# Second batch's expert blocks sorted on the chip by first tile; its output tiles added and stored between later blocks

## The chip, the cores and the metric

One Trainium2 chip, one core. The metric is the device time of the kernel in microseconds; before the change it is 1344.52 (median of 3 runs, 1341.7 to 1344.9). TensorE (PE in the profile) does matrix products, VectorE (DVE) and ScalarE (ACT) elementwise work, GpSimd (POOL) issues indirect DMAs here, and SyncE (SP) issues most of the plain DMAs.

## What is computed

Two layers over two images of 256 channels and 56 x 56 pixels, so N = 3136 tokens per batch. The first is a linear-attention convolution block; the second is causal attention and a mixture of experts. Only the last part is touched:

```python
def _L1_ffn_ref(x, gate_w, gate_b, W1, b1, W2, b2):
    xf = x.reshape(-1, Dd)
    logits = xf @ gate_w + gate_b
    probs = jax.nn.softmax(logits, axis=-1)
    top2_vals, top2_idx = jax.lax.top_k(probs, 2)
    cw = jnp.zeros((N, Ee), dtype=xf.dtype).at[jnp.arange(N)[:, None], top2_idx].add(top2_vals)
    def step(acc, params):
        w1, bb1, w2, bb2, we = params
        h = jax.nn.gelu(xf @ w1 + bb1, approximate=False)
        y = h @ w2 + bb2
        return (acc + we[:, None] * y, None)
    out, _ = jax.lax.scan(step, jnp.zeros_like(xf), (W1, b1, W2, b2, cw.T))
    return out.reshape(Bb, Tt, Dd)
...
t = t + _L1_ffn_ref(_ln_t(t), ...)
x = _from_tokens(t, x)
```

There are 8 experts, of hidden width 512. Each token goes to two experts, and the two outputs are added with their weights to the token. The result is written with channels ahead of pixels, so each tile of 128 tokens is transposed.

## The kernel before

**Pairs, slots, blocks.** A batch has 25 tiles of 128 tokens (the last has 64). A token with one of its experts is a pair: 6272 a batch. `dispatch(b)` (L923) works out on the chip where each pair goes: pairs are sorted by expert and, within an expert, by token, into slots; 128 slots are a block with one expert. There are 105 blocks (`NBLK`). Blocks 0 to 41 (below `FULL0`) are surely full of batch 0; blocks up to 56 (below `MIXED` = 57) may hold pairs of both; the rest is batch 1's. `dispatch` ends with a table of each block's expert (`eblks`) and of its bias (`b1bs`), L1073 to L1118, sets `ranked`, and then scatters normalised token rows into the slots in DRAM (`x_slots`) by indirect DMAs from GpSimd (L1135), 50 a batch.

**The block loop.** `experts` (L1151) runs the 105 blocks in a pipeline written out by hand: for iteration n it fetches the rows of a group of three blocks six blocks ahead (L1164, one DMA, SyncE), works out two blocks ahead where each row's result goes (`load`, L1177: `eq`, `to`), does the hidden layer of block n (L1236, L1245), the transposes of block n + 1 (L1213, L1217), copies the expert's first weights (L1224), and the output product of block n - 3 (L1255, L1265). Its result `ys` is stored by slot (`y_slots`, L1270) for blocks below 57, and scattered by token (`y_tokens`, L1272, GpSimd) for blocks from 42 on.

**Work between blocks.** At the end of each iteration `between` calls `pull`, which takes steps from jobs in a queue, the first job that has something to do first: two steps per block, three while batch 1's rows are being scattered. The jobs are `tokens` (projection, then `dispatch`), `closing` (which ends the attention's pools and runs `judge`, a check of the softmax sums), and, once block 56 has been worked, `finish(0)`. The program order of each engine is the order in which these steps are written.

**The end of a batch.** `finish(b)` (L1310) goes over 13 pairs of tiles: `fetch` gets the two experts' outputs `y0`, `y1` (for batch 0 by four indirect gathers from `y_slots`, L1334; for batch 1 by two plain loads from `y_tokens`, L1329), `add` adds them with their weights (L1349, four operations), `store` transposes (L1361), copies (L1366) and writes out (L1367; SyncE's queue for batch 0, ScalarE's for batch 1). `finish(1)` runs after all blocks, in a pool of its own, with 13 buffers. The rows it loads lie in `y_tokens` by token, and in the slot order each tile's rows come from blocks of every expert, the last expert's among them.

Of the kernel before, what the change touches and what calls it, by code (L numbers as in the profile page):

```python
# [9 lines left out]
F32 = mybir.dt.float32  # L10
U32 = mybir.dt.uint32
I32 = mybir.dt.int32
# [15 lines left out]
def conv_attn_moe_kernel(  # L28
# [18 lines left out]
    out: bass.AP,  # L47
):


# [25 lines left out]
    nc = tc.nc  # L76
# [275 lines left out]
    for c in range(NH):  # L352
# [36 lines left out]
        allow_small_or_imprecise_dtypes=True,  # L389
    )  # L390
    mixed_start = const.tile([P, E], F32, name="mixed_start")
    nc.gpsimd.iota(
# [34 lines left out]
    def layer1(nm, general):  # L427

        with ExitStack() as whole:
# [493 lines left out]
            def dispatch(b):  # L923
# [137 lines left out]
                for k in range(2):  # L1061
# [8 lines left out]
                    yield from small_piece()  # L1070


                s, e = (0, MIXED) if b == 0 else known[1]  # L1073
                if b == 1:
                    nc.vector.tensor_tensor(upto, upto, nfull.to_broadcast([P, E]), ALU.add)
                    nc.vector.tensor_scalar(upto, upto, float(E), None, ALU.add)
                past = g1.tile([P, e - s, E], F32, tag="blk", name=f"past_{nm}{b}")
                nc.vector.tensor_tensor(
                    past,
                    number[:, s:e].unsqueeze(2).to_broadcast([P, e - s, E]),  # L1080
                    upto.unsqueeze(1).to_broadcast([P, e - s, E]),
                    ALU.is_ge,
                )
                eb = g1.tile([P, e - s], F32, tag="eb", name=f"eb_{nm}{b}")
                nc.vector.tensor_reduce(eb, past, AX.X, ALU.add)
                yield from small_piece()
                if b == 0:
                    step = g1.tile([P, MIXED], F32, tag="step", name=f"step_{nm}{b}")
                    nc.vector.tensor_scalar(step, number[:, :MIXED], nfull, -float(E), ALU.is_ge, ALU.mult)
                    nc.vector.tensor_tensor(eb, eb, step, ALU.add)  # L1090
                    nc.vector.tensor_scalar(step, number[:, :MIXED], nfull, 0.0, ALU.subtract, ALU.max)
                    nc.vector.tensor_tensor(early, eb, step, ALU.add)
                    eb = early
                else:
                    nc.vector.tensor_scalar(eb, eb, float(E - 1), None, ALU.min)
                    step = g1.tile([P, MIXED - FULL0], F32, tag="step", name=f"step_{nm}{b}")
                    edge = few("edge")
                    nc.vector.tensor_scalar(edge[:, :1], nfull, float(E), None, ALU.add)
                    nc.vector.scalar_tensor_tensor(
                        step, number[:, FULL0:MIXED], edge[:, :1], early[:, FULL0:], ALU.is_lt, ALU.mult  # L1100
                    )
                    nc.vector.tensor_tensor(
                        eb[:, : MIXED - FULL0], eb[:, : MIXED - FULL0], step, ALU.add
                    )
                w = known[b][1] - known[b][0]
                nc.vector.tensor_copy(eblks[b], eb[:, :w])

                hot = g1.tile([E, w], F32, tag="hot", name=f"hot_{nm}{b}")
                nc.vector.tensor_tensor(hot, eb[:E, :w], row.to_broadcast([E, w]), ALU.is_equal)
                yield from small_piece()  # L1110
                for _ in range(1 if b else 3):
                    yield True
                bp = bank(f"bp_{b}", (P, KH, w))
                for k in range(KH):
                    nc.tensor.matmul(bp[:, k, :], b1s[:, k, :], hot, start=True, stop=True)
                nc.vector.tensor_copy(b1bs[b], bp)
                yield from small_piece()
                ranked[b] = True  # L1118
                while b and not scatter_rows:
# [31 lines left out]
            def experts(w1s, w2s, b2s, ex, es, ps6, between, need, written):  # L1151
# [4 lines left out]
                def fetch(g):  # L1156
                    s, e = g * GB, (g + 1) * GB
                    b = 0 if e <= FULL0 else 1
                    need(b)
                    if g == 0:  # L1160
                        return early_rows, None
                    f = known[b][0]
                    xb = ex.tile([P, GB, xds[b].shape[1]], F32, tag="xb", bufs=3, name=f"xb_{nm}_{g}")
                    (nc.sync if g > 2 else nc.scalar).dma_start(  # L1164
                        out=xb, in_=xds[b][(s - f) * P : (e - f) * P].rearrange("(n p) w -> p n w", p=P)
                    )
                    mixed = max(0, min(e, MIXED) - s) if b else 0
                    other = None
                    if mixed:
                        other = ex.tile([P, GB, C], F32, tag="xo", bufs=1, name=f"xo_{nm}_{g}")  # L1170
                        nc.sync.dma_start(
                            out=other[:, :mixed],
                            in_=xds[0][s * P : (s + mixed) * P].rearrange("(n p) w -> p n w", p=P),
                        )
                    return xb, other

                def load(g, xb, other):  # L1177
# [3 lines left out]
                    if b:  # L1181

                        eq = es.tile([P, GB], F32, tag="eq", name=f"eq_{nm}_{g}")
                        nc.vector.tensor_tensor(eq, xb[:, :, C + 1], slot_id[:, s:e], ALU.is_equal)
                        nc.vector.tensor_scalar(eq, eq, -float(N), float(N + OFF), ALU.mult, ALU.add)
# [64 lines left out]
                def outputs(n, state):  # L1250
# [20 lines left out]
                    if n >= FULL0:  # L1271
# [11 lines left out]
                        tc.declare_no_dep(s.ins, group=group, reason="different rows")  # L1283
                        tc.add_to_no_dep_group(group, s.ins)
                    if n == MIXED - 1:
                        written()
# [23 lines left out]
            def finish(b, oy, bufs):  # L1310
# [3 lines left out]
                def fetch(n, m, k):  # L1314

                    ys = [
                        oy.tile([P, 2, C], F32, tag=f"y{c}", bufs=bufs, name=f"y{c}_{nm}{b}_{n}")
                        for c in range(2)
                    ]
                    rows = t[:k, n : n + m, :C]  # L1320
                    if b == 0:
                        res = oy.tile([P, 2, C], F32, tag="res", bufs=bufs + 1, name=f"res_{nm}_{n}")
                        rows = res[:k, :m]
                        nc.sync.dma_start(out=rows, in_=rest_d[:k, n : n + m])
                    ahead.append((n, m, k, ys, rows))
                    for c, y in enumerate(ys):
                        r = c * N + n * P
                        if b:
                            nc.sync.dma_start(  # L1329
                                out=y[:k, :m],  # L1330
                                in_=y_tokens[r : r + (m - 1) * P + k].rearrange("(n p) d -> p n d", p=k),
                            )
                        for a in range(0 if b else m):
                            nc.gpsimd.indirect_dma_start(  # L1334
# [8 lines left out]
                            )  # L1343
                            yield True

                def add(n, m, k, ys, rows):
# [8 lines left out]
                def store(n, m, k, ys, rows):  # L1355
# [3 lines left out]
                    for o in range(NH):  # L1359
# [6 lines left out]
                    nc.scalar.copy(ot[:, :, :w], yo[:, :, :w])  # L1366
                    (nc.sync, nc.scalar)[b].dma_start(  # L1367
                        out=out[b, :, n * P : n * P + w].rearrange("(c p) n -> p c n", p=P),
# [4 lines left out]
                parts = deque(pairs())  # L1373
                while parts or ahead:
                    if parts:
                        yield from fetch(*parts.popleft())
                    if len(ahead) == bufs or not parts:
# [5 lines left out]
                        added = now  # L1383
                store(*added)

# [32 lines left out]

            projected, ranked, sent = ([False] * B for _ in range(3))
            first, early_rows, scatter_rows = [], [], []  # L1420
# [133 lines left out]
            def closing():  # L1554

                if not general:
# [5 lines left out]
                    while not projected[B - 1]:  # L1562
                        yield False
                    yield from judge()
                end.close()
# [4 lines left out]
            with ExitStack() as moe:  # L1570
# [17 lines left out]
                def need(b):  # L1588
                    while not sent[b]:
                        pull()  # L1590

                def written():
                    spread_rows.close()
                    oy = pool(moe, "oy", bufs=2, side="right")
                    queue.append(finish(0, oy, 2))

                with tc.manual_schedule(engines={PE, DVE, POOL, SP, ACT}):
                    experts(
                        first[0], w2s, b2s, ex, es, ps6,
                        lambda: pull(3 if ranked[1] and not sent[1] else 2), need, written,  # L1600
                    )
                while queue:
                    pull()
            early_w.close()
            with ExitStack() as last:
                oy = pool(last, "oz", bufs=2)
                for _ in finish(1, oy, 13):
                    pass

# [67 lines left out]
```

## Time and profile before

| | us |
|---|---|
| median of 3 runs | 1344.52 |
| profiled execution, span | 1375.5 |
| TensorE busy / VectorE / ScalarE / GpSimd | 1299.2 / 787.8 / 613.9 / 311.3 |
| block 0, copy of its transposed rows (L1217) | 884.63 |
| block 42 | 1071.35 |
| block 61 | 1142.25 |
| block 104, the last | 1321.46 |
| scatters of batch 1's rows, first and last start | 968.43, 1049.93 |
| first and last output store of batch 1, issued | 1340.73, 1370.33 |

Reading it: the copy at L1217 occurs once per block, so differences of its starts are the time of a block. A group's busy time is summed over the whole execution; the idle time beside it is that of the engine just before the group's instructions. Loads of registers and the issue of DMAs aren't counted as busy.

### The profile page before, as it was taken

The numbers are of one execution on the slowest core, as the hardware profiler recorded it, in microseconds if no ns is written. First come the engines' busy times: TensorE is split into PE (matmuls) and PEld (weight loads), VectorE is DVE, ScalarE is ACT, GpSimd is POOL, SyncE is SP. The second block draws the span as 40 slices with busy tenths as digits, with TensorE's granted clock in tenths as the row PEclk, the third lists the DMA queues.
The fourth block names the chain that finished last, engine by engine and source line by source line (L and its number), as shares of the span: only waits on it lengthen the run. The fifth ranks groups of instructions, "written<-read, shape, count | busy, mean of one in ns | idle before, by whom it ended". The sixth has DMA issues, their size and how long they took to land. (4 is left out here: it accounts for less than half of the span.)

```text
span 1375.5 us, 27937 instructions
## 1 busy us (share of the span) xinstructions
PE 1299.2 (94%) x10642; PEld 819.4 (60%) x10642; DVE 787.8 (57%) x1634; ACT 613.9 (45%) x1247; POOL 311.3 (23%) x299
## 2 busy tenths in 40 slices
PE   8999999999999999999999999999888998999973
PEld 7875444444444444434444444488878998999962
DVE  1572555757777455568587878647333443444435
ACT  0245555555565554555544565543223332343321
POOL 1113110000000221100043440000563125555530
PEclk9999999999999999999999999999999999999995
DMA  9992000000000001000011124411433334444427
GB/s 300 383 315 99 23 19 26 24 16 16 16 9 23 8 2 36 11 15 10 14 54 51 52 92 169 134 46 62 131 131 117 105 108 129 122 146 134 128 85 242
DMA packets 110373, 123.94 MB, mean 90 GB/s; under 512 B 19423, under 2 KB 99948, under 8 KB 110232
## 3 DMA queue, kind: packets, MB, share of 16 engines
q1 hardware_dynamic: 92456, 89.67, 21.5%
q0 software_dynamic: 10416, 26.00, 5.5%
q10 hardware_dynamic: 7360, 6.39, 1.4%
q8 instruction: 88, 1.44, 0.4%
q14 instruction: 53, 0.43, 0.1%
HBM read 63.04 MB, written 60.81 MB: 90 GB/s over the span
## 5 line engine op out<-in xcount | busy, mean ns | idle before, releaser
L645 ACT ACTIVATE st_f<-sc_f 128x896 f32<-128x896 f32 (+5 forms) x400 | 333.9, 838 | 291.9 <-PE sc_f L637 255.2
L659 DVE TENSOR_TENSOR acc_f<-acc_f,st_f 128x896 f32<-128x896 f32 (+5 forms) x372 | 366.6, 986 | 166.5 <-ACT st_f L645 157.9
L677 PE MATMUL yp_f<-st_f,v_f 64*64 64x448 f32 (+6 forms) x3184 | 341.0, 504 | 7.8 <-DVE qT_f L688 6.6
L637 PE MATMUL sc_f<-qT_f,kT_f 64*64 64x448 f32 (+6 forms) x3184 | 341.3, 500 | 0.0
L1236 PE MATMUL ht_f<-xT_f,w_f 128*128 128x128 f32 x1680 | 213.0, 281 | 27.0 <-ACT xT_f L1217 17.4
L1245 ACT ACTIVATE g_f<-ht_f,b1b 128x128 f32<-128x128 f32 x420 | 120.1, 369 | 265.1 <-PE ht_f L1236 158.2
L1236 PEld LDWEIGHTS ht_f<-xT_f,w_f 128*128 128x128 f32 x1680 | 206.3, 196 | 40.0 <-ACT xT_f L1217 25.2
L637 PEld LDWEIGHTS sc_f<-qT_f,kT_f 64*64 64x64 f32 x3184 | 117.1, 133 | 151.2 <-issue 136.7
L677 PEld LDWEIGHTS yp_f<-st_f,v_f 64*64 64x64 f32 x3184 | 111.3, 133 | 159.2 <-issue 131.3
L485 POOL TENSOR_SCALAR xn_f<-t 128x256 f32<-128x256 f32 (+1 forms) x50 | 67.3, 1355 | 548.1 <-issue 333.5
L1135 POOL DMA_INDIRECT x_slots<-xr_f,idx x100 | 114.1, 1141 | 247.2 <-DVE xr_f L1127 138.1
L1224 DVE COPY w_f<-w1s_f 128x1024 f32 x105 | 73.4, 699 | 94.4 <-PE ht_f L1236 47.2
L1265 DVE TENSOR_TENSOR ys_f<-yp_f,kT_f 128x128 f32<-128x128 f32 x105 | 30.6, 291 | 122.9 <-PE yp_f L1255 91.6
L1272 POOL DMA_INDIRECT y_tokens<-ys_f,to_f x63 | 63.8, 1013 | 145.3 <-DVE ys_f L1265 137.0
L523 PE MATMUL qk_f<-px_f,wat 128*128 128x512 f32 (+1 forms) x224 | 92.4, 558 | 1.2 <-ACT px_f L508 1.2
L647 DVE TENSOR_TENSOR st_f<-st_f,keep 128x256 f32<-128x256 f32 (+1 forms) x112 | 44.2, 395 | 64.8 <-ACT st_f L645 64.3
L523 PEld LDWEIGHTS qk_f<-px_f,wat 128*128 128x128 f32 x224 | 38.6, 190 | 54.3 <-issue 44.8
L1255 PE MATMUL yp_f<-px_f,g_f 128*128 x210 | 63.6, 385 | 0.0
L1255 PE MATMUL yp_f<-kT_f,g_f 128*128 x210 | 63.2, 383 | 0.0
L1255 PE MATMUL yp_f<-v_f,g_f 128*128 x210 | 62.6, 380 | 0.0
L1255 PE MATMUL yp_f<-w2s_f,g_f 128*128 x210 | 62.5, 379 | 0.0
L1334 POOL DMA_INDIRECT y_f<-y_slots,idx x50 | 56.5, 1131 | 16.3 <-issue 15.0
(217 smaller groups left out, 1177.5 us busy)
## 6 DMA issues: line engine op xcount, KB each, us to landing
x_slots<-fill SPq DMA_DIRECT2D x1, 8127.0 KB
xb_f<-x_slots SPq DMA_DIRECT2D x21, 387.0 KB
x_slots<-fill SPq DMA_DIRECT2D x1, 7296.0 KB
y_slots<-ys_f SPq DMA_DIRECT2D x57, 128.0 KB
kept<-t SPq DMA_DIRECT2D x2, 3200.0 KB
x<-in_x_dram SPq DMA_DIRECT2D x14, 448.0 KB
xr<-in_x_rows_dram SPq DMA_DIRECT2D x12, 512.0 KB
y_f<-y_tokens SPq DMA_DIRECT2D x24, 256.0 KB
```

Of the source, the lines that this page charges most:

```text
L485: nc.gpsimd.tensor_scalar(xn[:k, a], ts[b][:k, n + a, :C], ts[b][:k, n + a, MEAN : MEAN + 1], ts[b][:k, n + a, RSTD : RSTD + 1], ALU.subtr ...
L523: nc.tensor.matmul(ps[:, :w], wat[:, c, d0 : d0 + P], xT[:, c, :w], start=(c == 0), stop=(c == NH - 1),)
L637: nc.tensor.matmul(ps[h : h + HS, a, c0:W], kT[hp][rows, j * P + h : j * P + h + HS], qT[rows, hp, q0 + c0 : q0 + W], start=True, stop=True,)
L645: nc.scalar.activation(st[:k, :, c0:], ps[:k, :, c0:W], AF.Exp, scale=SCALE)
L659: nc.vector.tensor_tensor(acc[:k, :, c0:], acc[:k, :, c0:], st[:k, :, c0:], ALU.add)
L677: nc.tensor.matmul(yp[a * HS : (a + 1) * HS, h // HS, c0:W], v[hp][h : h + HS, j, a, :HS], st[h : h + HS, a, c0:], start=first, stop=bool( ...
L1135: s = nc.gpsimd.indirect_dma_start(out=xds[b], out_offset=bass.IndirectOffsetOnAxis(ap=idxs[b][:kk, k, n : n + 1], axis=0), in_=xr[:kk], i ...
L1224: nc.vector.tensor_copy(w, w1s[:, :, bass.ds(e, 1), :].rearrange("p c e h -> p c (e h)"))
L1236: nc.tensor.matmul(ht[:, k, :], w[:, c, k * P : (k + 1) * P], xT[:, c, :], start=(c == 0), stop=(c == NH - 1),)
L1245: nc.scalar.activation(g[:, k, :], ht[:, k, :], AF.Gelu, bias=b1bs[b][:, k, i : i + 1])
L1255: nc.tensor.matmul(yp[:, :C], g[:, k, :], w2s[k][:, bass.ds(e, 1), :].rearrange("p e d -> p (e d)"), start=(k == 0), stop=(k == KH - 1),)
L1272: s = nc.gpsimd.indirect_dma_start(out=y_tokens, out_offset=bass.IndirectOffsetOnAxis(ap=to[:, n % GB : n % GB + 1], axis=0), in_=ys, in_o ...
```

## The change

Four things are done.

1. `dispatch(1)` no longer builds the block table in line. It hands a job, `last_blocks`, to a list `side`, of which one step is taken per block besides the steps of `pull`, and goes on to scatter rows. `last_blocks` computes for each of the 63 blocks from 42 on the tile of its first pair, turns this into a key (blocks of the mixed region first, in their old order; blocks past the end last), ranks the keys, and permutes the table of experts. It keeps `qblk`, which place in `x_slots` the block at each position has, and `sid`, its slots' numbers.
2. The fetch of rows for batch 1 loads three places into SyncE's registers and issues three DMAs, one per block, in place of one.
3. `finish(1)` runs in the block loop, ahead of `finish(0)` in the queue, with 3 buffers. A pair of tiles is loaded when two more blocks have been worked than `complete` says; added two blocks after its load; stored a block after its adds. What is left after block 104 follows at once. The loads are declared independent of scatters of blocks that can't hold their rows. Its stores go by SyncE's queue. `pull` takes three steps per block once 57 blocks have been worked.
4. `judge` becomes a job at the end of the queue.

```diff
+def one_hot(eb, w):
+    nc.vector.tensor_copy(eblks[b], eb[:, :w])
...
+def last_blocks():
+    R = NBLK - FULL0
+    FAR = 1.0e5
...
+    nc.vector.tensor_scalar(
+        before, tot[:R].rearrange("p e t -> p (e t)"), rank, None, ALU.is_le
+    )
+    yield True
+    key, expert, own_part = (col(f"c_{k}") for k in ("key", "expert", "own"))
+    nc.vector.tensor_reduce(key, before, AX.X, ALU.add)
+    nc.vector.tensor_reduce(expert, past, AX.X, ALU.add)
+    nc.vector.scalar_tensor_tensor(key, expert, -float(NCH), key, ALU.mult, ALU.add)
...
+    keys = bank("keys", (P, 512))
+    nc.tensor.transpose(keys[:R, :R], key.to_broadcast([R, R]), ident[:R, :R])
+    less = small("one0").rearrange("p t e -> p (t e)")[:R, :R]
+    nc.vector.tensor_scalar(less, keys[:R, :R], key, None, ALU.is_lt)
+    nc.vector.tensor_reduce(rank, less, AX.X, ALU.add)
+    move = small("one1").rearrange("p t e -> p (t e)")[:R, :R]
+    nc.vector.tensor_scalar(move, number[:R, :R], rank, None, ALU.is_equal)
...
+    moved = bank("moved", (P, 2, R))
+    for k, c in enumerate((expert, own[:R])):
+        nc.tensor.matmul(moved[:, k], c.to_broadcast([R, P]), move, start=True, stop=True)
...
+    nc.vector.tensor_copy(qblk, moved[:, 1])
...
+if b == 0:
+    yield from first_blocks()
+else:
+    side.append(last_blocks())
+placed[b] = True
...
-(nc.sync if g > 2 else nc.scalar).dma_start(
-    out=xb, in_=xds[b][(s - f) * P : (e - f) * P].rearrange("(n p) w -> p n w", p=P)
-)
+if b:
+    at = nc.values_load_multi_w_load_instructions(
+        qblk[0:1, s - f : e - f], engines=(SP,), ...
+    )[1]
+    table = xds[b].rearrange("(n p) w -> n p w", p=P)
+    for a in range(GB):
+        nc.sync.dma_start(
+            out=xb[:, a],
+            in_=table[bass.ds(at[a], 1)].rearrange("o p w -> p (o w)"),
+        )
...
+def complete(n):
+    return min(NBLK, (2 * N + 2 * n * P) // P + E)
+
+def load(n, m, k):
...
+        i = nc.sync.dma_start(
+            out=y[:k, :m],
+            in_=y_tokens[r : r + (m - 1) * P + k].rearrange("(n p) d -> p n d", p=k),
+        ).ins
+        for block, other in scattered:
+            if block >= complete(n + m):
+                tc.declare_no_dep(i, other, reason="different rows")
...
-    (nc.sync, nc.scalar)[b].dma_start(
+    nc.sync.dma_start(
...
+GAP = 2
+while parts or ahead or added:
+    now = worked[0]
+    over = now == NBLK
+    if parts and len(ahead) < bufs:
+        n, m, k = parts[0]
+        if over or now >= complete(n + m) + GAP:
+            ahead.append((now, load(*parts.popleft())))
+            yield True
+            continue
+    if added and (over or now > added[0]):
+        store(*added[1])
+        added = None
+        yield True
+    elif ahead and not added and (over or now >= ahead[0][0] + GAP):
+        yield from add(*ahead[0][1])
+        added = now, ahead.popleft()[1]
+    else:
+        yield False
...
-    yield from judge()
+    queue.append(judge())
...
+def meanwhile():
+    scatters = placed[1] and not sent[1]
+    pull(3 if scatters or worked[0] >= MIXED else 2)
+    if side and next(side[0], None) is None:
+        side.popleft()
...
-with ExitStack() as last:
-    oy = pool(last, "oz", bufs=2)
-    for _ in finish(1, oy, 13):
-        pass
```

## The prediction

> **What bounds the kernel now.** I read the page's first two parts, then the engine times by stage, then the timeline of the end, then the waits of SyncE's queue there. The page's chain of waits is no help: it holds only the last three pieces, all on ScalarE and its queue. The stages say more (window, its length, then busy time of each engine with its count of instructions, the granted clock, the DMA share and GB/s):
>
> ```profile
> 1100.00:1150.00 50.00, 49.97 (x347) 46.83 (x346) 18.55 (x52) 18.30 (x66) 16.04 (x17) 1.00 0.42 128
> 1200.00:1250.00 50.00, 48.47 (x339) 44.83 (x338) 23.84 (x67) 20.19 (x68) 27.99 (x26) 1.00 0.47 143
> 1340.00:1375.50 35.50, 13.48 (x47) 7.95 (x46) 19.44 (x46) 7.30 (x13) 0.00 (x0) 0.50 0.77 245
> ```
>
> While expert blocks run, TensorE (first figure) is full and everything else has room. In the last window TensorE is idle for most of the time, at half clock, and DMA is busy 77%. So there are two limits: TensorE sets the block loop, and a chain of transfers sets the end. The timeline of the end shows that chain:
>
> ```profile
> 1331.85 0.97 POOL L1272 DMA_INDIRECT y_tokens<-ys_f,to_f  x1 [0.75 <-DVE ys_f L1265]
> 1334.67 6.65 SPq L1329 DMA_DIRECT2D y_f<-y_tokens  x10
> 1337.45 1.67 DVE L1349 SCALAR_TENSOR_TENSOR t<-y_f,wt,t 128x256 f32<-128x256 f32 x4 [5.88 <-DMA y_f<-y_tokens]
> 1338.78 1.30 PE L1361 MATMUL yo_f<-ident,t 128*128 128x128 f32 x4 [7.73 <-DVE t L1349]
> 1340.73 0.39 ACTq L1367 DMA_DIRECT2D out_dram<-ot_f  x1
> ...
> 1370.33 0.48 ACTq L1367 DMA_DIRECT2D out_dram<-ot_f  x1
> ```
>
> The last expert matmul ends at about 1331.05 (its last row starts at 1330.67 and lasts 0.38). The last scatter follows, then all 13 pairs of output tiles of batch 1 are loaded, added, transposed and stored. The first pair leaves at 1340.73, the thirteenth at 1370.33, and the span ends at 1375.50. The tail is 1375.50 - 1331.05 = 44.45 us. SyncE's queue shows why it cannot begin sooner: its first load waits for the scatters.
>
> ```profile
> SPq L1329 <- DMA y_tokens<-ys_f,to_f: 14.7, 1, 14.7
> ```
>
> In the block loop one ScalarE copy (L1217) marks each block. An undisturbed block, and then one that carries a store of batch 0:
>
> ```profile
> 1086.28 0.39 ACT L1217 COPY xT_f<-tp_f 128x256 f32<-128x256 f32 x1
> 1090.01 0.39 ACT L1217 COPY xT_f<-tp_f 128x256 f32<-128x256 f32 x1
> ...
> 1296.81 0.39 ACT L1217 COPY xT_f<-tp_f 128x256 f32<-128x256 f32 x1
> 1301.65 0.39 ACT L1217 COPY xT_f<-tp_f 128x256 f32<-128x256 f32 x1
> ```
>
> These are 3.73 us and 4.84 us.
>
> **What the Trainium skill says.** "DMA: Bandwidth & Descriptors", Anatomy of one DMA: a DMA from GpSimd has about 2.0 us of fixed cost, most of it the confirmation that the last byte has landed. The trace agrees: 2.82 us from the last scatter's start to the first load. This hop stays. The same page, Issuing engines are not separate DMA queues: all queues share 16 engines, so the output moved from ScalarE's queue to SyncE's saves no transfer time. No line here tests that alone. "TensorE: Matmul & The Clock Gate", What's actually happening: after an idle window of about 3.4 us TensorE runs at half clock. Here, the 16 hidden-layer matmuls of a block take 1.95 us, and 3.78 us after an idle of 3.06 us at 1162.24. A stall is therefore paid twice.
>
> **The change part by part.**
>
> (a) *Tail.* I followed the schedule by hand: 57 blocks are worked when both finish jobs start; a pair n, n+1 counts as complete at 49 + 2(n+2) + 8 blocks, is loaded 2 blocks later, added 2 after that, stored 1 after that. So pairs 0 to 18 (ten) are stored by block 102 of 105. Pair 20 is loaded at 103 and added and stored after the last block; pairs 22 and 24 are loaded after it. New tail, on the old time axis: the loads of pair 22 issue at 1334.67 as now, since they wait for the last scatter. Pair 20 lies in SBUF and is added and transposed in the gap of 5.88 us that VectorE now has. Pair 22 takes the place of today's first pair: out at 1340.73. Pair 24 has 64 rows and one tile: two more adds (about 0.48 each), two transposes (0.65), a copy (0.27), so out at about 1341.7. From the last store's issue to the end is 1375.50 - 1370.33 = 5.17 us and stays. New tail 1346.9 - 1331.05 = 15.8; **gain 28.6 us**. It could be 25 (SyncE issues four loads and three stores in order, at 0.38 to 0.48 each) to 30.
>
> (b) *Ten stores in the block loop.* Their transposes leave a stage where TensorE idles and enter one where it is full. Price: from block 69 (copy at 1179.90) to block 99 (1301.65) there are 30 blocks in 121.75 us; undisturbed they take 30 x 3.73 = 111.9; nine stores lie between, so (121.75 - 111.9)/9 = 1.09 us each, 0.6 to 0.9 of it TensorE's own and the rest what else a pair brings. **Ten cost 10.9 us.** Ends: 6 (transposes alone) and 16 (half as much again, where two pairs meet). The forty adds beside them (0.48 each, 19.2 us) lie on VectorE, which is busy 23.84 of 50 us; no block gets more than four, 1.9 us. The loads, 512 KB a pair, and stores, 256 KB, come to some 50 GB/s over 160 us beside 143; DMA share 0.47 leaves room.
>
> (c) *Three calls per block rather than two once 57 blocks are worked.* Batch 0's gathers come closer in the first blocks: up to three beside a scatter, at about 1.3 us from start to start, 5.2 us on GpSimd against a block of 3.73. Today, blocks 61 to 69 already take 37.65 us for 29.8 with two gathers a block. I take **+2 us**, 0 to 6.
>
> (d) *The order of the blocks.* Some forty small VectorE operations (0.15 to 0.6 us, about 9 us), a step per block over a dozen blocks, in place of two of 0.68 and a few more; VectorE is busy 23.95 of 50 us there. TensorE gets one transpose and two small products more; judge's two matmuls took 0.19 together, so under 1 us. **+1 us**, 0 to 3. Blocks copy their expert's weights in any order, so the order itself costs nothing.
>
> (e) *Row loads by a looked-up place.* Per group of three blocks SyncE gets one load of three registers and three DMAs for one. The register load is not in this trace for SyncE; the DMA page, Latency and other measured facts, puts a `tensor_load` at some 600 ns at least. With two more issues (0.39 each) I estimate 1.4 us, 3 at most, per 11.2 us. Queued behind them are SyncE's stores and later loads. It hides: the group loaded at 1117.99 is read by VectorE after 1130, and SyncE mostly waits. **0**, bounds 0 and 3.
>
> (f) *Waits of the early loads.* Each of SyncE's new loads waits for the scatter of a block issued two blocks back, 7.5 us, against 2.8 us of landing; behind it are row loads that have ten microseconds in hand. **0**, bounds 0 and 4.
>
> (g) *judge moved behind the dispatch, and the scatters of rows no longer behind the block table.* They begin some four blocks sooner. Block 42, their first reader, shows no wait now (blocks 41 to 43 are 3.73 apart), so **0**; if fewer of them met the loop it could gain 3.
>
> Sum: -28.6 + 10.9 + 2 + 1 = **-14.7 us** on a span of 1375.5. The profiled execution is 31 us longer than the median of the others, 1344.52; I take the difference over as it is (2% of it is nothing) and forecast **1330**.
>
> **Rivals.** *The loop gives it back.* Two or three more stalls of TensorE from the denser GpSimd and DMA work would leave 1341 to 1348. For it: blocks 65 to 67. Against it: from block 69 on, gathers, scatters and stores run together with no large stall. *Slower: a stall for every other early load.* Place: blocks 62 to 104. Price: blocks 65 to 67 took 7.24 + 5.28 + 4.92 = 17.4 us for 11.2, so 6.2 us for one stall with its cold clock. It decides from 14.7/6.2 = 2.4 stalls on; with five, 1344.5 - 14.7 + 31 = 1361. Against it is the same quiet stretch, and that VectorE's waiting is for data loaded two blocks earlier. *The change doesn't do what it says*: if each early load is made to wait for scatters that come later than those it needs, the pairs slip by a block or two, one more reaches the tail at some 1.5 to 2.5 us, and the result is about 1333. That lies in the forecast's range. *More gain*: if the earlier scatters stall the loop less and the stores pay only TensorE's 6 us, -28.6 + 6 + 1 - 3 = -24.6, 1320.
>
> **How the numbers follow.** Forecast with the slipped pairs 0.76 (1322 to 1338, from the ends above, not all at once), more gain 0.05, given back 0.08, slower 0.11. A difference of 0.3% is 4 us, about what a measurement can tell. Faster 0.81, same 0.08, slower 0.11. The range is 1318 to 1341: below it half of the extra gain, above it most of the last two cases.
>
> **What would show it.** Right: some 16 us from the last expert matmul to the end, three pairs' stores in it, and blocks 62 to 99 at about 4.4 us on average. Wrong: blocks of 6 to 7 us with TensorE waiting for xT after an early load; a block 42 that waits for its rows; a tail above 25 us.

## The result, and the profile after

| | median us | range |
|---|---|---|
| before | 1344.15 | 1341.7 to 1344.9 (4 runs) |
| after | 1324.13 | 1323.78 to 1325.2 (4 runs) |

The ratio is 0.9856, with a 95% interval of 0.9838 to 0.9873: the change takes 20.0 us off, where 14.7 were forecast.

One thing has to be known first. The chips used here fall in two kinds. On two of them ("prompt" below) the kernel before has medians of 1343.1 and 1343.7 us (all runs 1341.5 to 1347.5), on two others ("late") 1378.4 and 1378.2 (1375.8 to 1384.7). By its times, the comparison above is from a prompt chip; the profile of before that the prediction read, of 1375.5 us, has a late one's block loop (436.8 us from block 0 to 104, against 439.8 on a late and 403.8 on a prompt chip). The kernel before was therefore profiled again on a prompt chip; the comparison of traces uses that one (span 1342.3) beside the change (span 1323.5). The engine times by stage, before on a late chip (b0_again):

```profile
1150.00:1200.00 50.00, 43.78 (x291) 40.37 (x291) 19.70 (x54) 15.80 (x56) 26.55 (x26) 0.97 0.41 125
```

and the same kernel and window on a prompt chip (b0_third), with the last one:

```profile
1150.00:1200.00 50.00, 50.00 (x354) 47.17 (x353) 22.60 (x64) 20.60 (x69) 31.84 (x28) 1.00 0.49 151
...
1300.00:1342.30 42.30, 14.75 (x50) 8.63 (x50) 21.21 (x50) 7.30 (x13) 0.05 (x1) 0.52 0.73 231
```

TensorE (first figure after the length) is idle for 6.2 us of the first window on the late chip and never on the prompt one. The last window has the long tail on both. After the change, on a prompt chip:

```profile
1150.00:1200.00 50.00, 50.00 (x354) 46.98 (x353) 28.92 (x81) 22.27 (x72) 33.60 (x31) 1.00 0.69 213
1200.00:1250.00 50.00, 50.00 (x357) 47.15 (x357) 29.69 (x81) 21.41 (x71) 29.14 (x27) 1.00 0.60 184
...
1300.00:1323.50 23.50, 6.81 (x31) 5.00 (x29) 5.75 (x16) 1.39 (x3) 3.57 (x4) 0.67 0.30 91
```

TensorE stays full in the loop with VectorE at 29 of 50 us rather than 23 and DMA at 0.6 to 0.7 rather than 0.5: the loads and sums of the pairs of tiles fit beside the blocks, and only their transposes lengthen them (3.9 and 0.4 us in the table below). The end shrinks to one short window. Its timeline, before on the prompt chip:

```profile
1297.68 0.59 PE L1255 MATMUL yp_f<-w2s_f,g_f 128*128 x2
1299.07 0.97 POOL L1272 DMA_INDIRECT y_tokens<-ys_f,to_f  x1 [0.76 <-DVE ys_f L1265]
1301.90 28.26 SPq L1329 DMA_DIRECT2D y_f<-y_tokens  x26
...
1337.35 0.38 ACTq L1367 DMA_DIRECT2D out_dram<-ot_f  x1
```

and after:

```profile
1298.72 0.60 PE L1477 MATMUL yo_f<-ident,t 128*128 128x128 f32 x4
...
1299.97 0.38 SPq L1483 DMA_DIRECT2D out_dram<-ot_f  x1
...
1303.90 0.60 PE L1354 MATMUL yp_f<-w2s_f,g_f 128*128 x2
1305.64 0.97 POOL L1371 DMA_INDIRECT y_tokens<-ys_f,to_f  x1 [1.09 <-DVE ys_f L1364]
1306.33 0.66 PE L1477 MATMUL yo_f<-ident,t 128*128 128x128 f32 x4 [1.83 <-DVE t L1465]
1307.68 0.38 SPq L1483 DMA_DIRECT2D out_dram<-ot_f  x1
1308.52 2.54 SPq L1452 DMA_DIRECT2D y_f<-y_tokens  x4
1311.48 2.57 DVE L1465 SCALAR_TENSOR_TENSOR t<-y_f,wt,t 128x256 f32<-128x256 f32 x6 [5.21 <-DMA y_f<-y_tokens]
...
1314.81 1.06 SPq L1483 DMA_DIRECT2D out_dram<-ot_f  x2
```

Before, 26 loads stand behind the last scatter and the thirteenth store is issued at 1337.35. After, four loads do; the first two rows are pair 18, the tenth that goes in the loop, pair 20 is stored at 1307.68 and pairs 22 and 24 in the last row. From the end of the last expert matmul (1298.27 and 1304.50) to the end of the span it was 44.0 us and is 19.0.

The whole difference of the two spans, by the copies that mark the blocks:

| stretch | before | after | change |
|---|---|---|---|
| start to block 0 | 884.86 | 886.11 | +1.25 |
| block 0 to 61 | 237.63 | 238.23 | +0.60 |
| block 61 to 104 | 166.19 | 170.13 | +3.94 |
| block 104 to the last expert matmul's end | 9.59 | 10.03 | +0.44 |
| to the end of the span | 44.03 | 19.00 | -25.03 |
| span | 1342.3 | 1323.5 | -18.8 |

### The profile page after: what moved, and what is told of

Same layout as the page of the kernel before. It is cut to its first block, busy times and chain, and to the rows that moved or that the text cites. A ratio compares the mean times of both kernels' runs of the same rounds, so it can differ in the third digit from the quotient of the medians.

```text
span 1323.5 us, 28216 instructions
## 1 busy us (share of the span) xinstructions
PE 1281.4 (97%) x10647; PEld 811.4 (61%) x10647; DVE 791.9 (60%) x1657; ACT 613.2 (46%) x1247; POOL 311.8 (24%) x300
## 4 chain that ended last, share of the span: by engine, by line
PE 92%; DVE 2%; ACT 2%; DMA 1%; issue 1%; POOL 1%; SPq 0%; DVEq 0%; ACTq 0%; POOLq 0%
PE yp_f L689 21%; PE sc_f L649 19%; PE ht_f L1335 14%; PE yp_f L1354 13%; PE qk_f L535 6%; PE pp_f L598 4%; PE v_f L554 4%; PE cp L321 3%; PE gram L252 3%; PE tp_f L1312 2%; ACT st_f L657 1%; PE sp_f L716 1%; PE yo_f L1477 1%; DVE acc_f L671 1%; PE xp_f L514 1%
## 5 line engine op out<-in xcount | busy, mean ns | idle before, releaser
L1335 PE MATMUL ht_f<-xT_f,w_f 128*128 128x128 f32 x1680 | 205.8, 276 | 5.8 <-ACT xT_f L1316 5.8
L1335 PEld LDWEIGHTS ht_f<-xT_f,w_f 128*128 128x128 f32 x1680 | 201.6, 192 | 12.5 <-ACT xT_f L1316 7.7
L1364 DVE TENSOR_TENSOR ys_f<-yp_f,kT_f 128x128 f32<-128x128 f32 x105 | 30.5, 291 | 102.8 <-PE yp_f L1354 102.7
```

The costliest lines, as they stand in the source:

```text
L1335: nc.tensor.matmul(ht[:, k, :], w[:, c, k * P : (k + 1) * P], xT[:, c, :], start=(c == 0), stop=(c == NH - 1),)
```

## The experiments

Each expectation names its own theories. Two theories were at stake at first. One: the gain is the shorter tail, less what the ten stores take from TensorE in the loop. The rival: the order of the blocks and the closer DMAs cost in the loop what they do, and the tail's gain would be had in another way too. The two kinds of chip then put a third question: what a late chip loses time on. One late chip ran the kernel before, order alone, the ten pairs left out and the eight held; the other ran the kernel before, the change, both distances and the spread gathers. The kernel before differs by 0.2 us between these two.

| kernel | prompt chip, us | late chip, us |
|---|---|---|
| before | 1344.15, 1343.10, 1343.68 | 1378.44, 1378.24 |
| the change | 1324.13 | 1362.34 |
| order alone, no early finish | 1341.89 | 1384.61 |
| ten pairs left out | | 1360.35 |
| eight pairs held until the end | | 1363.27 |
| distance of no block, of one block | | 1432.88, 1362.29 |
| gathers spread | 1324.83 | 1349.40 |
| gathers and row scatters spread | 1325.25 | |

**The kernel before, on both kinds of chip.**

> The kernel before, unchanged, profiled once more. Theory 1 (the stalls of TensorE in the first profile belong to that one execution, which was 31 us longer than the timed ones): span about 1342, blocks 0 to 104 in 402 to 406 us instead of 436.8, no block of 5 us or more after block 20, and a store of batch 0 costs about 0.44 us of a block as a store of either batch does in the profile after. Theory 2 (the kernel before stalls in this way each time, and the change takes the stalls away): span about 1375, blocks 0 to 104 in about 437 us, blocks of 5 to 7.6 us during the scatters of rows.

> The kernel before, unchanged, profiled once more. If it takes about 1344 here: blocks 0 to 104 in 402 to 406 us with no block of 5 us or more after block 20, and 0.44 us for a store of batch 0. If it takes about 1378: as in its two other profiles, blocks 0 to 104 in 437 to 440 us.

It took 1379.98 and 1344.05 us. From block 0 to block 104 the late chip needs 439.81 us, the prompt one 403.82; the tails are alike (52.31 and 53.62 from block 104 on). So the 36 us between the two profiles lie in the loop, and nearly all in two stages: blocks 18 to 42 exceed 24 x 3.73 us by 22.3 on the late chip and 1.3 on the prompt one, blocks 61 to 104 exceed 43 x 3.73 by 20.1 and 5.8. In both stages GpSimd issues several indirect DMAs a block. Between them, from block 42 to 61, it issues one, and the excess is 0.04 us on the late chip too.

**The change, on a late chip.**

> The changed kernel once more, beside the kernel before. In the comparison before was 1344 and this 1324; in the first experiments before was 1378 and the block loop of every kernel had blocks of 5 to 10 us wherever GpSimd issues indirect DMAs back to back, so the chips differ. If before is about 1344 here: 1324 (-20). If before is about 1378: tail -25.4, ten stores +4.4, closer gathers +6 (what the order alone showed) = -15, so 1363; if on the contrary the early loads and stores add stalls of their own, above 1370.

It took 1362.34 us, ratio 0.9868 (0.9835 to 0.9902): 15.9 us faster, not 20. The loop costs more there (444.85 us, 5.0 more than before), the tail falls as on the prompt chip. One of its worst blocks in the timeline:

```profile
1147.70 2.05 PE L1335 MATMUL ht_f<-xT_f,w_f 128*128 128x128 f32 x16 [0.69 <-ACT xT_f L1316]
...
1150.78 1.00 POOL L1427 DMA_INDIRECT y_f<-y_slots,idx  x1 [0.30 <-issue]
1151.10 0.59 PE L1354 MATMUL yp_f<-w2s_f,g_f 128*128 x2
1152.08 1.03 POOL L1371 DMA_INDIRECT y_tokens<-ys_f,to_f  x1 [0.31 <-issue]
1153.42 1.02 POOL L1427 DMA_INDIRECT y_f<-y_slots,idx  x1 [0.31 <-issue]
1154.74 1.01 POOL L1427 DMA_INDIRECT y_f<-y_slots,idx  x1 [0.30 <-issue]
1157.02 1.15 ACT L1344 ACTIVATE g_f<-ht_f,b1b 128x128 f32<-128x128 f32 x4 [9.38 <-remote]
1157.02 0.69 DVE L1323 COPY w_f<-w1s_f 128x1024 f32 x1 [5.72 <-remote]
...
1158.48 3.78 PE L1335 MATMUL ht_f<-xT_f,w_f 128*128 128x128 f32 x16 [6.79 <-ACT xT_f L1316]
```

The hidden-layer product that ScalarE and VectorE wait for is recorded as done at 1149.75. Both start together at 1157.02, 7.3 us later, and 1.3 us after GpSimd's run of DMAs ends. TensorE then waits 6.79 us for ScalarE's copy and does the next product at half clock, 3.78 us for 1.95. That agrees with "TensorE: Matmul & The Clock Gate", What's actually happening, in the Trainium skill, and it is why a stall is paid twice. The prediction's own case, 3.78 us after an idle of 3.06 in the trace of before, stands behind a shorter idle than the 3.4 us that it took from that page, so 3.4 is no sure lower limit here. The ends of matmuls are modelled, so the trace doesn't say whether the product or its signal was late.

**Undo the early finish, keep the order.** Batch 1's pairs are all finished after the last block, with 13 buffers and on ScalarE's queue as before.

```diff
-                    queue.appendleft(finish(1, oy, 3))
...
+            with ExitStack() as last:
+                oy = pool(last, "oz", bufs=2)
+                for _ in finish(1, oy, 13):
+                    pass
```

> The change without its early finish: order on the chip, loads by looked-up place, judge moved, three steps per block, but batch 1 is finished after the last block with 13 buffers by ScalarE's queue, as before. Theory 1: the whole gain is the shorter end, so this is 1345, 0 to 3 us above before (the forecast had +1 for the order, +2 for the closer gathers). Theory 2: moving the scatters ahead of the block table is what ends the stalls, so this is about 1325 to 1332.

> The change without its early finish, as in e1_order_only: order of blocks by first tile, but batch 1's pairs all loaded, added and stored after the last block, on ScalarE's queue. Theory 1 (what the order costs depends on the chip: it packs the indirect DMAs closer, and only a chip where TensorE's signals come late under them loses by it): if the kernel before takes some 1344 us here, this kernel takes 1344 to 1346, the order of blocks costing about 1 us, with no block of 5 us or more after block 61; if the kernel before takes some 1378 us here, 1384 again. Theory 2 (the order's own work on VectorE and SyncE costs the 6 us): 1349 to 1351 where the kernel before takes 1344, and 1384 where it takes 1378.

On the late chip it took 1384.61 us, ratio 1.0040 (1.0020 to 1.0059), on a prompt one 1341.89, ratio 0.9987 (0.9980 to 0.9994). The same code is 6.2 us slower than before on one and 1.8 us faster on the other. Its busy times, on the late chip:

```profile
1150.00:1200.00 50.00, 40.48 (x260) 36.56 (x259) 20.24 (x56) 15.42 (x52) 30.16 (x29) 0.93 0.46 143
```

and on the prompt one:

```profile
1150.00:1200.00 50.00, 50.00 (x354) 47.07 (x353) 27.36 (x77) 21.10 (x70) 39.32 (x36) 1.00 0.61 186
```

The prompt chip gets through 36 GpSimd instructions in the window (the last count), with TensorE full; the late one through 29, with TensorE idle for 9.5 us. On the prompt chip the loop is 2.0 us longer than before and the start 1.0; the tail is 5.2 us shorter, which neither theory had (the least that was expected is 1344): the loads that can't touch the last blocks' rows don't wait for the last scatter.

```profile
1299.97 28.68 SPq L1452 DMA_DIRECT2D y_f<-y_tokens  x26
...
1302.04 0.97 POOL L1371 DMA_INDIRECT y_tokens<-ys_f,to_f  x1 [0.76 <-DVE ys_f L1364]
```

They begin 2.1 us ahead of it, where before they began 2.8 us behind it. Why they don't begin sooner wasn't tried. It fits that their buffers lie in a pool that is opened when the blocks' own is closed; SyncE's longest wait there is for TensorE:

```profile
SPq L1452 <- PE yp_f L1354: 41.0, 1, 41.0
```

Another point was missed: no block of 5 us or more was expected after block 61, but blocks 88 and 89, at the end of batch 0's work, take 5.21 and 5.08. VectorE waits there for gathers, 1.85 and 1.97 us.

So the order alone is worth 1.8 us on a prompt chip and the change 20.0; the other 18 come with finishing pairs in the loop, in buffers that are free there.

**Ten pairs left out; eight held until the end.** In the first kernel tiles 0 to 19 of batch 1 are never loaded, added or written, so its output lacks them. In the second they keep their place up to tile 9, and the other pairs wait for the last block.

```diff
-                parts = deque(pairs())
+                parts = deque(pairs(20 if b else 0))
```

```diff
-                        if over or now >= complete(n + m) + GAP:
+                        if over or (n < 10 and now >= complete(n + m) + GAP):
```

> The change with batch 1's first ten pairs of tiles (0 to 18) left out: they are neither loaded, added, transposed nor written, so the output lacks them; pairs 20 to 24 are finished as in the change. The difference to the changed kernel is what ten pairs cost inside the block loop. Theory 1 (four transposes each, nothing else): 4.4 us, so 1319.7. The forecast's price of 1.09 us each: 10.9 us, so 1313.2.

> The change with only the first five pairs finished in the block loop; the other eight wait until the last block. Each pair moved back costs the tail 2.47 us (the step from store to store in the tail before) and frees the loop of 0.44 us (theory 1) or 1.09 us (forecast): 5 x 2.03 = +10.2 us, so 1334.3, or 5 x 1.38 = +6.9, so 1331. If three buffers are too few for the tail's loads, it is above 1336.

Left out: 1360.35 us (1359.31 to 1361.97), 2.0 us less than the change on a late chip (1358.08 to 1363.53), with ranges that overlap. Blocks 61 to 104 exceed 43 x 3.73 us by 31.6 without the ten pairs and by 30.2 with them: in a loop that stalls already, they cost nothing that can be seen, and neither 4.4 nor 10.9 us is confirmed. Nor do they cause its stalls: order alone, with no pair of batch 1 in the loop, exceeds by 31.3 there. What ten pairs cost a loop that doesn't stall is read from the blocks on a prompt chip, further below; leaving them out wasn't tried on one. Held: 1363.27 us, within 1 us of the change, where some 7 to 10 more was expected. The timeline of its end shows what the expectation missed:

```profile
1303.49 19.65 SPq L1452 DMA_DIRECT2D y_f<-y_tokens  x10
1306.42 1.68 DVE L1465 SCALAR_TENSOR_TENSOR t<-y_f,wt,t 128x256 f32<-128x256 f32 x4 [0.41 <-DMA y_f<-y_tokens]
...
1308.01 0.28 DVE L1364 TENSOR_TENSOR ys_f<-yp_f,kT_f 128x128 f32<-128x128 f32 x1
...
1343.12 0.89 SPq L1483 DMA_DIRECT2D out_dram<-ot_f  x2
1343.37 0.97 POOL L1371 DMA_INDIRECT y_tokens<-ys_f,to_f  x1 [0.30 <-issue]
...
1346.93 0.88 SPq L1452 DMA_DIRECT2D y_f<-y_tokens  x2
```

Eight pairs are held. Block 104's copy is at 1332.44, but the first held pair is loaded at 1303.49 and added at 1306.42: the loads wait for no late scatter, so SyncE and VectorE do them beside the last blocks. The edit puts them behind the last block, but the adds of 1306.42 stand ahead of a block's own sum (L1364) at 1308.01. What is written behind the block loop thus doesn't have to run behind it: unlike in the loop, the order of an engine isn't that of the steps there, and this kernel holds back no more than transposes and stores. By 1341.42 six of the eight are added. Their transposes and stores are what is left, and they fall into the wait for the last scatter and the last two pairs' loads, so that the tail from block 104 on is 29.56 us for 28.88. So a store at its own block isn't what the gain needs. What both kernels have in common is that only two pairs depend on the last scatters and that the others are loaded and added before. A kernel that truly holds back the loads and adds wasn't run.

**The distance between a block's scatter and the load.** `GAP` is 2 in the change; 0 and 1 were tried.

> The change with no distance between a tile's completion, its load and its adds (GAP 0 in place of 2). Then VectorE's adds stand right behind the load, which waits for a scatter just issued: scatter 1.0, landing 2.8, load 2.9 us, with VectorE in order behind. If the distance of two blocks is what hides the early loads' waits: 3 to 5 us a pair for ten or eleven pairs, so 30 to 50 us slower than the change. If the waits hide in any case (the forecast's 0 for them needs no distance): within 3 us of the change.

> The change with a distance of one block in place of two. One block is 3.73 us, against 2.9 us for a load and up to 4 us for the scatter that it waits for. If one block is enough: within 2 us of the change (the pair that moves from the tail into the loop, pair 20, lay in the wait for the last scatter anyway). If not: 1 to 2 us a pair, 10 to 20 us slower.

Without distance: 1432.88 us, ratio 1.0382 (1.0336 to 1.0429), 70.5 us more than the change, where 30 to 50 was expected. With one block: 1362.29, as the change. The longest waits of VectorE and of TensorE without distance, from 1145 to 1300 us:

```profile
DVE t L1465 <- DMA y_f<-y_tokens: 39.6, 12, 7.4
```

```profile
PE yo_f L1477 <- DVE t L1465: 28.0, 12, 5.5
```

VectorE's adds wait twelve times for a load that waits for a scatter just issued, up to 7.4 us, and TensorE's transposes wait for the adds. All that comes behind in those two engines' order, the next expert product too, stands. With one or two blocks of distance this wait isn't among VectorE's six costliest. It is the prediction's slower rival with nearly its price: from block 65 on every fourth block, ten in all, takes 9.2 to 12.1 us, together 72 us more than 3.73 each, so 7.2 a stall where 6.2 was said. All this is from a late chip.

**The gathers of batch 0 spread out.** A late chip stalls where GpSimd issues indirect DMAs one after another. At most two gathers a block, and one in every third, from block 57 on; all else as in the change.

```diff
+                            while gathers[0] == 0:
+                                yield False
+                            gathers[0] -= 1
                             nc.gpsimd.indirect_dma_start(
...
+                    gathers[0] = 2 - (worked[0] % 3 == 0)
                     pull(3 if scatters or worked[0] >= MIXED else 2)
```

> The change with at most two gathers of batch 0 per block, and one in every third, instead of up to three; all of them still end within the block loop. If before is about 1378 here and dense issue on GpSimd is what stalls TensorE: 3 to 8 us faster than the change. If before is about 1344, or the stalls have nothing to do with how dense the gathers are: within 2 us of the change.

> The change with only the gathers spread, once more, on the same chip as the run with both spread. If before is about 1378 here: 1349 again. If before is about 1344: within 2 us of 1324, since there the gathers at up to three a block stall nothing.

On the late chip 1349.40 us, ratio 0.9797 (0.9762 to 0.9831), 12.9 less than the change on the same chip, where 3 to 8 was expected. Blocks 61 to 104 exceed 43 x 3.73 us by 15.1 instead of 30.2, and the window that the change fills with 39.83 us of TensorE has

```profile
1150.00:1200.00 50.00, 47.35 (x331) 43.92 (x330) 24.63 (x68) 18.09 (x61) 29.33 (x28) 1.00 0.53 162
```

On a prompt chip it took 1324.83, as the change. So gathers that come less closely take away half of the stalls of this stage on a late chip. Their adds and stores come less closely too, and no run parts the two; but blocks 18 to 42 stall as well, and the indirect DMAs there are scatters of rows. What holds the signal isn't shown.

**The row scatters spread too.** Three steps of `pull` only in every other block while batch 1's rows are scattered.

```diff
-                    pull(3 if scatters or worked[0] >= MIXED else 2)
+                    pull(3 if (scatters and worked[0] % 2) or worked[0] >= MIXED else 2)
```

> The change with the gathers spread as in the run before (two a block, one in every third) and with batch 1's row scatters taken at two and three steps of work per block alternately instead of three. If before is about 1378 here and a dense GpSimd queue is what stalls TensorE: another 3 to 10 us below the run with only the gathers spread, so 1340 to 1346. If the row scatters stall it at 2.5 a block as well, within 3 us of it. If before is about 1344: within 2 us of 1324 for both.

On a prompt chip 1325.25 us, no difference from the change; it wasn't run on a late one, so whether it would help there is open.

## Why the prediction was right, and where it was off

The direction and the mechanism were right: a tail of transfers was traded for work beside a full TensorE. The sum of -14.7 became -18.8 on the spans because its terms erred in both directions: the tail gave 3.6 us less than forecast, and the costs in the loop were 8.9 us smaller. That the two partly cancel is luck. The forecast also carried a difference worked out on a late profile over to prompt times.

- **(a) The tail**: 25.0, where 28.6 was forecast and 25 to 30 allowed. The steps up to the last stores came near what was worked out: last matmul to scatter 1.14 us (0.80), scatter to load 2.88 us (2.82), load to add 2.96 (2.78), add to the last issue 3.8 (4.25). The scatter comes later since VectorE does two of pair 20's adds ahead of the last block's sum. The step that failed is "from the last store's issue to the end is 5.17 us and stays". It took 8.2: the issue is at 1315.3, SyncE's last wait for a landing ends at about 1320.0, and then its closing instructions, with their waits for other engines, take the 3.5 us to 1323.5. Before, the last stores were on ScalarE's queue: ScalarE sees the landing at 1341.0, 1.3 us ahead of the end, and SyncE's closing lay beside that wait. The move of the last stores from ScalarE's queue to SyncE's was given no price; leaving them there in the change wasn't tried. But all profiles with these stores on ScalarE's queue, order alone included, take 4.7 to 5.2 us from the last issue to the end, and all with them on SyncE's 6.1 to 8.5. That supports the reading; the spread shows that the queue isn't all of it.
- **(b) Ten stores in the loop**: 4.4, where 10.9 was forecast and 6 to 16 allowed. This is the mis-sized term. The 1.09 us per store were an average over a stretch of a late chip's profile and held that chip's stalls: TensorE is idle there for 3.3 us, and the same thirty blocks of the same kernel take 115.46 us on a prompt chip instead of 121.75. (The prediction looked at windows on both sides of 1150 to 1200; in that one its profile has TensorE busy for 46.17 us of 50, at a clock of 0.93.) On the prompt chip a block with a store takes 0.44 us more, before and after alike; two neighbours in the change, the first with a store and the second without:

```profile
1282.84 0.39 ACT L1316 COPY xT_f<-tp_f 128x256 f32<-128x256 f32 x1
...
1287.01 0.39 ACT L1316 COPY xT_f<-tp_f 128x256 f32<-128x256 f32 x1
...
1290.74 0.39 ACT L1316 COPY xT_f<-tp_f 128x256 f32<-128x256 f32 x1
```

  4.17 and 3.73 us. Ten make 4.4. Nine lie between the copies of blocks 61 and 104, which are 3.94 us further apart than before; the tenth, pair 18's, is transposed at 1298.72, behind block 104's copy, and is the 0.44 us that the stretch behind that copy is longer in the table. The lower end of the range, "transposes alone", was too high too.
- **(c) Closer gathers**: 0 on the prompt chip, where blocks 57 to 65 are all 3.73 us; +2 was forecast. On a late chip they cost more than that: order alone, three calls a block with it, adds 11 us to the loop.
- **(d) The order, computed on the chip**: +0.6 between blocks 0 and 61, where +1 was forecast. Blocks 20, 22, 25 and 33 take 4.12, 4.51, 4.96 and 4.05 us; blocks ahead of 18, and 18 itself, got quicker.
- **(e) and (f)**: 0 as forecast. A group's register load takes 0.67 to 2.09 us on SyncE (0.86 in the middle) and its three DMA issues 1.39 to 2.65, more than the 1.4 us that was estimated. But TensorE never waits for the rows on the prompt chip; VectorE does so a few times, 0.7 us at most. The early loads' waits are hidden at a distance of two blocks, and at one.
- **(g)**: 0. On prompt chips the row scatters run from 953.0 to 1020.9 instead of 968.6 to 1035.6, and blocks 42 to 57 take 55.98 us, 15 x 3.73, in both.
- Not in the sum: +1.25 us ahead of block 0 (the same kernel differs by 2.0 there between two profiles).

Together: -14.7 + 3.6 (a) - 6.5 (b) - 2 (c) - 0.4 (d) + 1.2 (ahead of block 0) = -18.8. Of the signs named in advance, three pairs' stores lie in the tail as said; it is 19.0 us rather than some 16, below the 25 that would have meant wrong. Blocks 62 to 99 take 3.95 us on average, not 4.4. No block waits for an early load. The rival "more gain" at 1320 named the right reason, stores at TensorE's price alone, but the longer close took part of it back; its other reason, that earlier scatters stall the loop less, isn't seen (blocks 18 to 42 take 1.5 us more than before).

## What to carry to other kernels

A chain of transfers at the end shortens when the work is ordered so that only a few transfers depend on the last results, and when the others are declared free of them and have buffers in time. In these runs it was enough that the others' loads and sums, not their stores, lay ahead of the end. Put at least one step of distance between a write and a load of it that an in-order engine then waits for; here one block, 3.7 us, was as good as two. And when a profile is slower than the timed runs, see in which stage it is slower before taking prices from that stage.

## What was unexpected of the hardware

Two of the four chips of the experiments took 2.6% longer for the same kernel (1378.4 and 1343.7), nearly all of it in stages where GpSimd issues indirect DMAs back to back (blocks of up to 10.8 us instead of 3.73), and nothing where it issues one a block (0.04 us over 19 blocks). A ranking of two kernels turned round with the kind of chip: order alone was 6.2 us slower than before on one and 1.8 us faster on the other. Whether this belongs to the chip or to its condition on that day can't be told from these runs, and the mechanism stays open. A version with spread gathers costs nothing on a prompt chip and saves 12.9 us on a late one.
